# First batch of a two-layer graph network: where message work stands among the leaf products, and when the x parts of the quarters are put in

## The chip, the cores and the metric

The kernel runs on one core of one Trainium2 chip. The metric is device time in microseconds (us). Every kernel was run several times, always with runs of the kernel before on the same chip. PE is the matrix engine, DVE the vector engine, ACT the scalar engine, POOL the general-purpose engine. "Clock" is the clock that the throttle granted to PE, 1.00 being full speed.

## The reference, cut to what matters

There are 64 graphs of 256 nodes with 256 channels, all in fp32. Layer 0 adds three things into a gated unit: a convolution over the nodes (a 1-wide one, then a 17-wide one), a message pass, and the old state. Layer 1 (not touched here) normalises and aggregates over the adjacency.

```python
h = relu(bn(conv1d(xc, conv1_w, 0)))                  # xc: x with channels first
x_conv = transpose(relu(bn(conv1d(h, conv2_w, 8)) + xc))
s = x @ w_se.T + b_se                                 # 3 coordinates per node
A = exp(-squared_distances(s)) * mask                 # "distances", "mask"
msg = relu(x @ w_msg.T + b_msg)                       # "messages"
x_nmp = A @ msg                                       # "passing"
# r, z, n gates from concat(x_conv, x_nmp) and x; then layer 1
```

The 17-wide convolution is done for eight graphs (a batch) at a time by a transform: DVE splits the input into leaves, PE multiplies the leaves by transformed filters ("leaf products"), DVE merges the results back ("the way back", its additions and subtractions called butterflies in the code). The way back hands over its result in four parts, the quarters. PE transposes ("turns") each quarter into a pair of banks into which it has already put the old x of the same nodes (the "x part"). The convolution of a later batch is hidden among the gates of the batch before it. The first batch has nothing to hide among: its whole transform stands open at the start of the run, with the filters ahead of it. The change is about this opening.

## The kernel before

The parts that matter here are below. A leaf group takes three PSUM banks out of eight; `take` copies its sums away and frees them. The scheduler is manual: each engine runs its instructions in the order in which the program issues them.

```python
def products(b, first, sums):
    p1, p2, p3 = bank("ps_k1"), bank("ps_k2"), bank("ps_k3")
    ...                                        # 12 matmuls (24 records in the trace)
    def take():
        k1 = sl(sums, 2).rearrange("p s e -> p (s e)")
        nc.scalar.copy(k1, p1)                 # ACT, L395
        nc.vector.tensor_sub(..., k1, p3)      # DVE, L396
        nc.vector.tensor_add(..., k1, p2)      # DVE, L397
    return take

# in conv(b): the eight groups (four, two, one, "last")
for i, (make, after) in enumerate(todo):
    ...
    take = make()
    yield PE_WEIGHT                # before: early work is placed HERE, ahead of the take
    ...
    take()
    yield beyond * 2 * cost(2)
    if after and b == 0:
        yield from after           # the merges that follow this take, on DVE
    ...
STAGE[b] = "inverse"
...                                # butterflies (DVE)
if b == 0:
    def turned_x(q): ...           # PE puts x itself into the two banks of quarter q
    yield None
    held = [turned_x(0), turned_x(1)]
    for q in range(4):
        ...                        # second, third (DVE), then PE adds the turned quarter (L554)
        if q < 2:
            held.append(turned_x(q + 2))
        yield None
    return

def messages(k, idle=False):
    for m in range(C):
        ps = bank("ps_msg")
        for c in range(C):
            nc.tensor.matmul(ps[:, :D + 4], XT[k][:, c, m * P:(m + 1) * P], wms[:, c, :], ...)     # L626
        if idle:
            nc.tensor.matmul(ps[:, :D + 4], ones[0:1, :], bms[0:1, :], start=False, stop=True)     # L629
            nc.scalar.copy(twice[:, m, :, 0:3], ...)                                               # L630
            nc.scalar.activation(MSG[k][:, m, :], ps[:, :D], AF.Relu)                              # L631
    ...                                        # five small POOL operations

early = deque([lambda: messages(0, True), lambda: messages(1, True), lambda: factors(0), lambda: messages(2, True),
               lambda: distances(0), lambda: factors(1), lambda: distances(1)])
while STAGE.get(0) != "inverse":
    if next(first) == PE_WEIGHT and early:
        early.popleft()()
...
nc.gpsimd.tensor_add(brzn[:, :2 * D], brzn[:, :2 * D], bhh)
early.extend([lambda: mask(0), lambda: passing(0)])
for t in first:
    if t is None and early:
        early.popleft()()
mask(1)
```

`messages(k)` needs the transposed x of graph k, which was written to memory and is read back.

Of the kernel before, what the change touches and what calls it, by code (L numbers as in the profile page):

```python
# [16 lines left out]
P = 128  # L17
B, N, D = 64, 256, 256
C = D // P
# [9 lines left out]
M, T = 16, 32  # L29
# [15 lines left out]
PE_WEIGHT = 0.3  # L45
# [30 lines left out]
def gnn_two_layers(  # L76
# [17 lines left out]
    nc = tc.nc  # L94
# [4 lines left out]
    def bank(name):  # L99
        return psum.tile([P, 512], F32, tag="ps", name=name)  # L100
# [14 lines left out]
    def x_by_tiles(b, nodes, tag="xb"):  # L115

        t = conv_pool.tile([P, 4, D], F32, tag=tag, name="xb", bufs=2 if tag == "xb" else 1)
        nc.sync.dma_start(
            out=t, in_=x[b * BG:(b + 1) * BG].rearrange("g (t j) d -> (g t) j d", j=M)[:, nodes, :])
        return t  # L120
# [12 lines left out]
    ident = const.tile([P, P], F32)  # L133
# [32 lines left out]
    W2, FIRST = {}, {}  # L166
# [73 lines left out]
    def sl(a, n, step=1):  # L240
        return X[:, a:a + n] if step == 1 else X[:, a:a + (n - 1) * step + 1:step]

    def cost(n):

        return 0.15 + 0.265 * n
# [109 lines left out]
    def butterflies(pairs):  # L355
        for o, a, b, n, add in pairs:
            (nc.vector.tensor_add if add else nc.vector.tensor_sub)(sl(o, n), sl(a, n), sl(b, n))  # L357
            yield cost(n)
# [71 lines left out]
    def conv(b):  # L430
# [59 lines left out]
        for i, (make, after) in enumerate(todo):  # L490
            if i == 4:
                for t in other:
                    yield beyond * t
            take = make()
            yield PE_WEIGHT
            while vector and spent < share * (i + 1):
                t = next(vector[0], None)
                if t is None:
                    vector.popleft()
                else:  # L500
                    spent += t
                    yield beyond * t
            take()
            yield beyond * 2 * cost(2)
            if after and b == 0:
                yield from after
            elif after:
                vector.append(after)
        STAGE[b] = "inverse"
        for steps in vector:  # L510
            yield from steps
        sv, s8, s4 = sv[8, 0], s8[4, 0], s4[2, 0]
        yield from butterflies([(S2, U, U + 1, 1, True), (S2 + 1, U, U + 1, 1, False),
                                (U, S2, U + 2, 2, True), (U + 2, S2, U + 2, 2, False)])
        for j in range(2):
# [4 lines left out]
        def second(j):  # L520
            stt(sl(U + j, 2, 4), sl(U + 8 + j, 2, 4), s8[j], sl(S2 + j, 2, 4))
            yield cost(2)
            stt(sl(U + 8 + j, 2, 4), sl(U + 8 + j, 2, 4), -s8[j], sl(S2 + j, 2, 4))
            yield cost(2)
# [7 lines left out]
        for g in range(BG):  # L532
            XC[b * BG + g] = (xcs[g // 4], g % 4)
        if b == 0:

            def turned_x(q):
                xb = FIRST["xb"][q] if q < 3 else x_by_tiles(b, slice(q, M, 4))
                pss = [bank("ps_xc") for _ in range(C)]
                for o in range(C):
                    for j in range(4):  # L540
                        nc.tensor.matmul(pss[o][:, j * P:(j + 1) * P], xb[:, j, o * P:(o + 1) * P], ident,
                                         start=(j == 0), stop=False)
                return pss

            yield None
            held = [turned_x(0), turned_x(1)]
            for q in range(4):
                yield from second(q)
                yield from third(q)
                yield from third(q + 4)  # L550
                pss = held.pop(0)
                for o in range(C):
                    for j in range(4):
                        nc.tensor.matmul(pss[o][:, j * P:(j + 1) * P], X[:, V + q + 4 * j, o * P:(o + 1) * P], ident,  # L554
                                         start=False, stop=(j == 3))
                for o in range(C):
                    pv = pss[o].rearrange("p (j g t) -> p j g t", j=4, g=BG)
                    for h in range(2):
                        nc.scalar.activation(xcs[h][:, o].rearrange("p g (t j) -> p j g t", j=M)[:, q::4],
                                             pv[:, :, 4 * h:4 * h + 4, :], AF.Relu)  # L560
# [4 lines that stand above are left out]
# [18 lines left out]
        for q in range(4):  # L583
            xb = x_by_tiles(b, slice(4 * q, 4 * q + 4))
# [33 lines left out]
    def messages(k, idle=False):  # L618

        MSG[k] = ahead.tile([P, C, D], F32, tag="msg", name="msg", bufs=3)  # L620
        st = sts[k % len(sts)]
        twice = st.rearrange("p m (r e) -> p m r e", e=SR)
# [3 lines that stand above are left out]
                nc.tensor.matmul(ps[:, :D + 4], XT[k][:, c, m * P:(m + 1) * P], wms[:, c, :],  # L626
                                 start=(c == 0), stop=(c == C - 1 and not idle))
            if idle:
                nc.tensor.matmul(ps[:, :D + 4], ones[0:1, :], bms[0:1, :], start=False, stop=True)  # L629
                nc.scalar.copy(twice[:, m, :, 0:3], ps[:, D:D + 3].unsqueeze(1).to_broadcast([P, 2, 3]))  # L630
                nc.scalar.activation(MSG[k][:, m, :], ps[:, :D], AF.Relu)  # L631
                continue
            nc.vector.tensor_add(twice[:, m, :, 0:3], ps[:, D:D + 3].unsqueeze(1).to_broadcast([P, 2, 3]),
                                 bms[:, D:D + 3].unsqueeze(1).to_broadcast([P, 2, 3]))
            nc.vector.tensor_add(MSG[k][:, m, :], ps[:, :D], bms[:, :D])  # L635
        if not idle:
            nc.scalar.activation(MSG[k], MSG[k], AF.Relu)  # L637

        sq = ahead.tile([P, C, 3], F32, tag="sq", name="sq", bufs=2)
        ns = ahead.tile([P, C], F32, tag="ns", name="ns", bufs=3)  # L640
        nc.gpsimd.tensor_mul(sq, st[:, :, 0:3], st[:, :, 0:3])
        nc.gpsimd.tensor_add(ns, sq[:, :, 0], sq[:, :, 1])
        nc.gpsimd.tensor_add(ns, ns, sq[:, :, 2])
        nc.gpsimd.tensor_scalar(twice[:, :, :, 3], ns.unsqueeze(2).to_broadcast([P, C, 2]), -0.5, None, ALU.mult)
        nc.gpsimd.tensor_scalar(ns, ns, -1.0, None, ALU.mult)
        ST[k] = (st, ns)

    def factors(k):
        st, ns = ST[k]
        ps = bank("ps_sT")  # L650
        for m in range(C):
            nc.tensor.transpose(ps[:ROWS, m * P:(m + 1) * P], st[:, m, :ROWS], ident)
        lr = ahead.tile([ROWS, 2, N], F32, tag="lr", name="lr", bufs=1)
        nc.scalar.activation(lr[:, 0, :], ps[:ROWS, :N], AF.Identity, bias=lone[:, 1:2], scale=lone[:, 0:1])
        nc.scalar.copy(lr[:, 1, :], ps[:ROWS, :N])
        ST[k] = (lr, ns)

    def distances(k):
        lr, ns = ST[k]
        AT[k] = ahead.tile([P, C, N], F32, tag="AT", name="AT", bufs=2)  # L660
        pss = [bank("ps_dist") for _ in range(C)]
        for m in range(C):
            r = slice(m * SR, m * SR + 4)
            nc.tensor.matmul(pss[m][:, :N], lr[r, 0, m * P:(m + 1) * P], lr[r, 1, :], start=True, stop=True)
        for m in range(C):
            nc.scalar.activation(AT[k][:, m, :], pss[m][:, :N], AF.Exp, bias=ns[:, m:m + 1], scale=2.0)  # L666

    def mask(k):
        nc.vector.tensor_mul(AT[k], AT[k], ADJ[k])

    def passing(k):
        NMP[k] = work.tile([P, C, N], F32, tag="nmp", name="nmp")
        ps = bank("ps_nmp")
        for d in range(C):
            for m in range(C):
                nc.tensor.matmul(ps[:, d * N:(d + 1) * N], MSG[k][:, m, d * P:(d + 1) * P], AT[k][:, m, :],  # L676
                                 start=(m == 0), stop=(m == C - 1))
        nc.scalar.copy(NMP[k].rearrange("p c n -> p (c n)"), ps)
# [128 lines left out]
    first = conv(0)  # L807
# [69 lines left out]
    for k in range(3):  # L877
# [3 lines left out]
    nc.gpsimd.tensor_scalar(wrr, wrr, 0.5, None, ALU.mult)  # L881
    nc.gpsimd.tensor_scalar(brel, brel, 0.5, None, ALU.mult)

    early = deque([lambda: messages(0, True), lambda: messages(1, True), lambda: factors(0), lambda: messages(2, True),
                   lambda: distances(0), lambda: factors(1), lambda: distances(1)])
    while STAGE.get(0) != "inverse":
        if next(first) == PE_WEIGHT and early:
            early.popleft()()
    first_pool.close()

    work = ctx.enter_context(tc.tile_pool(name="work", bufs=2))
# [5 lines left out]
    nc.gpsimd.tensor_add(brzn[:, :2 * D], brzn[:, :2 * D], bhh)  # L897
    load_x(0)

    early.extend([lambda: mask(0), lambda: passing(0)])  # L900
    for t in first:
        if t is None and early:
            early.popleft()()
    mask(1)

    POINTS = 10
# [107 lines left out]
```

## Time and profile before

The opening, read from the timeline of the kernel before (us from the start of the span):

| point | us |
|---|---|
| first leaf product on PE | 80.71 |
| first take on DVE (group 0) | 99.57 |
| group 3's take on DVE | 124.54 |
| first turned quarter on PE | 163.31 |
| first gate product (L692) | 178.28 |
| total, median of the first three runs | 2303.77 |

From the first gate product on PE is nearly always busy, so the question of the change is how early that product starts. In the timeline each row is: start, length, engine, source line, operation, output<-inputs, shapes, number of instructions joined, and in brackets how long the engine stood idle before and what ended that. A chain row has start, length and what. A windows row has stretch, length, then busy time of PE, PEld, DVE, ACT and POOL, the clock, the DMA share and GB/s. One fp32 matmul shows as two records.

### The profile page before, as it was taken

The numbers are of one execution on the slowest core, as the hardware profiler recorded it, in microseconds if no ns is written. First come the engines' busy times: TensorE is split into PE (matmuls) and PEld (weight loads), VectorE is DVE, ScalarE is ACT, GpSimd is POOL, SyncE is SP. The second block draws the span as 40 slices with busy tenths as digits, with TensorE's granted clock in tenths as the row PEclk, the third lists the DMA queues.
The fourth block names the chain that finished last, engine by engine and source line by source line (L and its number), as shares of the span: only waits on it lengthen the run. The fifth ranks groups of instructions, "written<-read, shape, count | busy, mean of one in ns | idle before, by whom it ended". The sixth has DMA issues, their size and how long they took to land.

```text
span 2300.6 us, 24425 instructions
## 1 busy us (share of the span) xinstructions
PE 2230.2 (97%) x8370; PEld 1464.9 (64%) x8370; DVE 1678.8 (73%) x3188; ACT 766.4 (33%) x1585; POOL 464.7 (20%) x926
## 2 busy tenths in 40 slices
PE   8879999999999999999999999999999999999996
PEld 5665666666666666666766566666666666666663
DVE  6693988659893888839987597957889298874543
ACT  6414322442235322343224432243223532243332
POOL 0100312212122222203212121222222122121211
PEclk9889999999999999999999999999999999999998
DMA  5922242224332144222522243231432314321100
GB/s 145 310 83 78 92 144 86 86 71 142 106 96 96 47 133 137 74 97 61 175 71 81 96 133 120 73 110 51 137 121 86 101 37 154 112 79 37 46 23 14
DMA packets 212665, 226.68 MB, mean 99 GB/s; under 512 B 22087, under 2 KB 203838, under 8 KB 212542
## 3 DMA queue, kind: packets, MB, share of 16 engines
q1 hardware_dynamic: 189984, 191.14, 26.4%
q10 hardware_dynamic: 22558, 33.99, 4.2%
q8 instruction: 67, 1.10, 0.2%
q14 instruction: 56, 0.46, 0.1%
HBM read 179.22 MB, written 45.88 MB: 98 GB/s over the span
## 4 chain that ended last, share of the span: by engine, by line
PE 74%; DVE 19%; issue 2%; DMA 1%; POOL 1%; ACT 1%; SPq 1%; ACTq 0%; POOLq 0%; DVEq 0%
PE ps_rz L694 16%; PE ps_k L380 11%; PE ps_n L706 8%; PE ps_rz L692 8%; DVE XF L103 7%; PE ps_out L769 6%; PE ps_c L461 5%; PE ps_nmp L676 4%; PE ps_n L704 4%; PE ps_msg L626 4%; PE ps_out L781 3%; DVE w L103 2%; DVE bst L711 1%; DVE XF L427 1%; PE ps_xc L574 1%
## 5 line engine op out<-in xcount | busy, mean ns | idle before, releaser
L103 DVE SCALAR_TENSOR_TENSOR XF<-XF 128x512 f32<-128x512 f32 (+2 forms) x800 | 508.6, 666 | 7.4
L733 POOL TENSOR_SCALAR q<-mv 128x2 f32<-128x2 f32 x64 | 32.1, 501 | 1470.4 <-DVE mv L712 1470.4
L380 PE MATMUL ps_k<-w,XF 128*128 128x256 f32 x1316 | 301.8, 385 | 13.3 <-ACT AT L666 11.6
L380 PEld LDWEIGHTS ps_k<-w,XF 128*128 128x128 f32 x1316 | 248.7, 192 | 61.4 <-ACT AT L666 17.3
L707 DVE TENSOR_TENSOR gn<-ps_n,brzn 128x512 f32<-128x512 f32 x128 | 88.0, 688 | 239.0 <-PE ps_n L706 239.0
L698 ACT ACTIVATE rz<-rz 128x512 f32<-128x512 f32 x128 | 80.6, 630 | 508.8 <-DVE rz L697 508.8
L692 PE MATMUL ps_rz<-whh,xT 128*128 128x512 f32 x512 | 241.8, 595 | 0.0
L694 PE MATMUL ps_rz<-wih,xc 128*128 128x512 f32 x512 | 240.6, 592 | 0.0
L694 PE MATMUL ps_rz<-wih,nmp 128*128 128x512 f32 x512 | 240.6, 592 | 0.0
L769 PE MATMUL ps_out<-wrr,hT 128*128 128x512 f32 x512 | 231.9, 596 | 5.5 <-ACT hT L758 5.5
L697 DVE TENSOR_TENSOR rz<-ps_rz,brzn 128x512 f32<-128x512 f32 x128 | 87.1, 681 | 197.3 <-PE ps_rz L694 197.1
L694 PEld LDWEIGHTS ps_rz<-wih,xc 128*128 128x128 f32 x512 | 97.3, 190 | 122.5 <-issue 122.3
L694 PEld LDWEIGHTS ps_rz<-wih,nmp 128*128 128x128 f32 x512 | 97.3, 190 | 122.5 <-issue 122.5
L769 PEld LDWEIGHTS ps_out<-wrr,hT 128*128 128x128 f32 x512 | 97.8, 191 | 104.5 <-issue 89.2
L637 ACT ACTIVATE msg<-msg 128x512 f32<-128x512 f32 x61 | 38.4, 630 | 334.1 <-DVE msg L635 334.1
L626 PE MATMUL ps_msg<-wms,xT 128*128 128x260 f32 x512 | 133.6, 399 | 10.3 <-DMA w2m<-w2all 5.9
L692 PEld LDWEIGHTS ps_rz<-whh,xT 128*128 128x128 f32 x512 | 92.8, 191 | 65.0 <-issue 61.8
L704 PE MATMUL ps_n<-whh,xT 128*128 128x256 f32 x512 | 131.6, 379 | 0.0
L706 PE MATMUL ps_n<-wih,xc 128*128 128x256 f32 x512 | 131.4, 379 | 0.0
L706 PE MATMUL ps_n<-wih,nmp 128*128 128x256 f32 x512 | 131.4, 379 | 0.0
L357 DVE TENSOR_TENSOR XF<-XF 128x512 f32<-128x512 f32 (+3 forms) x128 | 125.3, 1004 | 1.7
L770 ACT COPY hr<-ps_out 128x256 f32<-128x256 f32 x128 | 47.6, 372 | 232.6 <-PE ps_out L769 232.6
(115 smaller groups left out, 3562.3 us busy)
## 6 DMA issues: line engine op xcount, KB each, us to landing
w<-w2m SPq DMA_DIRECT2D x105, 768.0 KB, 5.7
xn<-in_x_dram SPq DMA_DIRECT2D x32, 512.0 KB, 4.4
xt<-xTc ACTq DMA_DIRECT2D x32, 512.0 KB, 3.2
xT<-xt SPq DMA_DIRECT2D x64, 256.0 KB, 3.0
xb<-in_x_dram SPq DMA_DIRECT2D x32, 512.0 KB, 5.3
adj<-in_adjT_dram SPq DMA_DIRECT2D x64, 256.0 KB, 2.8
x<-in_x_dram SPq DMA_DIRECT2D x64, 256.0 KB, 3.0
out_dram<-y ACTq DMA_DIRECT2D x64, 256.0 KB, 2.2
```

The lines of the kernel that those rows point to most:

```text
L103: nc.vector.scalar_tensor_tensor(o, in0, s, in1, op0=op0, op1=op1)
L357: (nc.vector.tensor_add if add else nc.vector.tensor_sub)(sl(o, n), sl(a, n), sl(b, n))
L380: nc.tensor.matmul(ps, X[:, slot, c * P:(c + 1) * P], w(m, c), start=(c == 0), stop=(c == C - 1))
L461: nc.tensor.matmul(ps, w1[:, c, o * P:(o + 1) * P], xTc[:, c, :], start=(c == 0), stop=(c == C - 1))
L626: nc.tensor.matmul(ps[:, :D + 4], XT[k][:, c, m * P:(m + 1) * P], wms[:, c, :], start=(c == 0), stop=(c == C - 1 and not idle))
L676: nc.tensor.matmul(ps[:, d * N:(d + 1) * N], MSG[k][:, m, d * P:(d + 1) * P], AT[k][:, m, :], start=(m == 0), stop=(m == C - 1))
L692: nc.tensor.matmul(prz, XT[k][:, c, q], whh[:, c, 0:2 * D], start=(c == 0), stop=False)
L694: nc.tensor.matmul(prz, t, wih[:, i, 0:2 * D], start=False, stop=(i == 3))
L704: nc.tensor.matmul(pn[:, D:], XT[k][:, c, q], whh[:, c, 2 * D:], start=(c == 0), stop=(c == C - 1))
L706: nc.tensor.matmul(pn[:, :D], t, wih[:, i, 2 * D:], start=(i == 0), stop=(i == 3))
L707: nc.vector.tensor_add(RZ[k][1][:, n, :], pn, brzn[:, 2 * D:])
L769: nc.tensor.matmul(ps, hT[:, c, n * P:(n + 1) * P], wrr[:, c, :], start=(c == 0), stop=(c == C - 1))
```

## The change

The intent is that message work of the early graphs shall not stand in front of the leaf takes, on PE or on ACT. In numbers of groups: messages 0, messages 1, factors 0 and distances 0 go behind groups 1, 2, 3 and 4 instead of groups 0, 1, 2 and 4, and behind the take and its merges instead of ahead of it (factors is the small transpose that distances needs); messages 2, factors 1 and distances 1 go into the way back. The x parts of the first two quarters are issued ahead of the butterflies. No instruction is added or removed.

```diff
--- before.py
+++ after.py
@@ -502,14 +502,27 @@
                     yield beyond * t
             take()
             yield beyond * 2 * cost(2)
-            if after and b == 0:
-                yield from after
+            if b == 0:
+                yield from after or ()
+                yield None
             elif after:
                 vector.append(after)
         STAGE[b] = "inverse"
         for steps in vector:
             yield from steps
         sv, s8, s4 = sv[8, 0], s8[4, 0], s4[2, 0]
+        if b == 0:
+
+            def turned_x(q):
+                xb = FIRST["xb"][q] if q < 3 else x_by_tiles(b, slice(q, M, 4))
+                pss = [bank("ps_xc") for _ in range(C)]
+                for o in range(C):
+                    for j in range(4):
+                        nc.tensor.matmul(pss[o][:, j * P:(j + 1) * P], xb[:, j, o * P:(o + 1) * P], ident,
+                                         start=(j == 0), stop=False)
+                return pss
+
+            held = [turned_x(0), turned_x(1)]
         yield from butterflies([(S2, U, U + 1, 1, True), (S2 + 1, U, U + 1, 1, False),
                                 (U, S2, U + 2, 2, True), (U + 2, S2, U + 2, 2, False)])
         for j in range(2):
@@ -532,18 +545,6 @@
         for g in range(BG):
             XC[b * BG + g] = (xcs[g // 4], g % 4)
         if b == 0:
-
-            def turned_x(q):
-                xb = FIRST["xb"][q] if q < 3 else x_by_tiles(b, slice(q, M, 4))
-                pss = [bank("ps_xc") for _ in range(C)]
-                for o in range(C):
-                    for j in range(4):
-                        nc.tensor.matmul(pss[o][:, j * P:(j + 1) * P], xb[:, j, o * P:(o + 1) * P], ident,
-                                         start=(j == 0), stop=False)
-                return pss
-
-            yield None
-            held = [turned_x(0), turned_x(1)]
             for q in range(4):
                 yield from second(q)
                 yield from third(q)
@@ -881,11 +882,18 @@
     nc.gpsimd.tensor_scalar(wrr, wrr, 0.5, None, ALU.mult)
     nc.gpsimd.tensor_scalar(brel, brel, 0.5, None, ALU.mult)
 
-    early = deque([lambda: messages(0, True), lambda: messages(1, True), lambda: factors(0), lambda: messages(2, True),
-                   lambda: distances(0), lambda: factors(1), lambda: distances(1)])
+    count = 0
     while STAGE.get(0) != "inverse":
-        if next(first) == PE_WEIGHT and early:
-            early.popleft()()
+        if next(first) is None:
+            count += 1
+            if count == 2:
+                messages(0, True)
+            elif count == 3:
+                messages(1, True)
+            elif count == 4:
+                factors(0)
+            elif count == 5:
+                distances(0)
     first_pool.close()
 
     work = ctx.enter_context(tc.tile_pool(name="work", bufs=2))
@@ -897,10 +905,13 @@
     nc.gpsimd.tensor_add(brzn[:, :2 * D], brzn[:, :2 * D], bhh)
     load_x(0)
 
-    early.extend([lambda: mask(0), lambda: passing(0)])
-    for t in first:
-        if t is None and early:
-            early.popleft()()
+    early = {1: lambda: messages(2, True), 4: lambda: mask(0), 5: lambda: factors(1)}
+    later = deque([lambda: distances(1), lambda: passing(0)])
+    for i, t in enumerate(first):
+        if i in early:
+            early[i]()
+        if t is None and later:
+            later.popleft()()
     mask(1)
 
     POINTS = 10
```

In the changed kernel the lines have moved: L627 and L630 are the message matmuls (626 and 629 before), L521 the x parts (541), L555 the turned quarters (554), L693 the first gate product (692).

## The prediction

> **What bounds the kernel now.** I read the page's slices first. The matrix engine (PE) is over nine tenths busy from the fourth slice to the last but one, so nearly the whole run is PE work which this change leaves alone. Only the first three slices (57.5 us each, so to about 172 us) are below that, and there the granted clock falls too:
>
> ```profile
> PE   8879999999999999999999999999999999999996
> PEclk9889999999999999999999999999999999999998
> ```
>
> The order of instructions of the changed program, set against the old one, differs only inside this opening; the rest has the same instructions in the same order. So the question is by how much the first gate product (line 694's group; its first matmul, L692, starts at 178.44 us) comes sooner. The chain of waits, asked for 78 to 186 us, gives the opening in order (start, length, what):
>
> ```profile
> 80.42 10.73 DMA w2m<-w2all
> 91.15 1.00 issue
> 92.15 2.07 PE ps_msg L626 x4
> ...
> 121.84 1.07 PE ps_msg L626 x4
> 122.91 0.65 PE ps_msg L629 x2
> 123.58 0.16 ACT st L630
> 123.75 0.29 ACT msg L631
> 124.03 0.49 ACT XF L395
> 124.52 0.02 issue
> 124.54 0.69 DVE XF L396
> ...
> 163.31 3.96 PE ps_xc L554 x16
> ...
> 178.44 1.72 PE ps_rz L692 x4
> ```
>
> The reader should see three stretches. To 124 us the chain is PE with message work in it and a transfer ahead of it; then ScalarE (ACT) copies the messages before the leaf sums (L395); from 124.54 to 163.3 us the chain is VectorE (DVE) alone; then PE turns the quarters until the gates. The windows view shows what the transfer costs beyond its wait (stretch, length, PE busy, PEld, DVE, ACT, POOL, clock, DMA share, GB/s):
>
> ```profile
> 86.30:92.15 5.85, 0.00 (x0) 0.03 (x1) 2.79 (x4) 0.00 (x0) 0.00 (x0) 0.79 1.03 328
> 92.15:98.50 6.35, 6.35 (x12) 3.31 (x12) 0.00 (x0) 0.55 (x2) 0.00 (x0) 0.50 1.00 316
> 98.50:106.20 7.70, 7.70 (x26) 6.37 (x26) 3.43 (x6) 0.93 (x3) 1.03 (x5) 0.68 1.08 383
> 106.20:123.00 16.80, 16.80 (x74) 12.85 (x73) 10.51 (x16) 3.12 (x10) 1.04 (x5) 1.00 0.46 163
> ```
>
> PE stands 5.85 us for the first transposed x, then works at half clock. The timeline by engine adds that the first leaf sums, whose products ended at 86.29, were copied at 98.95 and used only then:
>
> ```profile
> 98.95 0.59 ACT L395 COPY XF<-ps_k 128x512 f32<-128x512 f32 x1
> 99.57 0.69 DVE L396 TENSOR_TENSOR XF<-XF,ps_k 128x512 f32<-128x512 f32 x1 [10.45 <-ACT XF L395]
> 110.55 0.69 DVE L396 TENSOR_TENSOR XF<-XF,ps_k 128x512 f32<-128x512 f32 x1 [7.44 <-ACT XF L395]
> 124.54 0.69 DVE L396 TENSOR_TENSOR XF<-XF,ps_k 128x512 f32<-128x512 f32 x1 [3.17 <-ACT XF L395]
> ```
>
> DVE loses 10.45 + 7.44 + 3.17 = 21.06 us to these three waits: the ceiling of the gain, if the rest of DVE's chain keeps its length.
>
> **What the Trainium skill says.** "TensorE: Matmul & The Clock Gate", part 1, says that PE's clock is halved after an idle window of about 3.4 us and full again after about as much work, with a free-running window. The trace agrees on the halving (0.50 after 5.85 us of idling, and message matmuls at about twice their later time) but PE stayed slow into the stretch after 98.5 us, longer than one such window. The same page, under the architectural detail, says that ScalarE and VectorE are strict FIFOs: this is why L395 stood behind message copies that had nothing to do with it, and 98.95 against 86.29 agrees. "PSUM — Partial Sum Buffer", the four rules: a matmul's output fits in one bank; with eight banks and three for each leaf group, PE can run ahead by only two groups before it needs DVE's take.
>
> **The change part by part.** I number the leaf groups 0 to 6, then the last. *Before*, PE ran group 0, message 0, group 1, message 1, group 2, factors 0, group 3, message 2 and so on. *After* it runs groups 0 and 1, message 0, group 2, message 1, group 3, factors 0, group 4, distances 0, groups 5, 6 and last, two x parts, then message 2 and factors 1; distances 1 and the first pass come among the quarters. Nothing is removed or added except order.
>
> 1. Groups 0 and 1. PE ends group 0 at 86.29 as before. A warm group is 5.35 us (24 records; 5.38 and 5.18 in the chain plus gaps), so group 1 ends at 91.64. Message 0 then finds its x nearly landed; I keep 92.15, a wait of 0.5 us, too short to cool the clock.
> 2. Message 0, warm: 106.34 to 109.55 in the chain, so 3.21 us: to 95.36. Group 2 to 100.71, message 1 to 103.92, group 3 to 109.27.
> 3. DVE starts at 89.12, the end of its last butterfly (three L357 from 86.96), as group 0's copy no longer has a message before it. A take with its small merges is 3.5 us (99.57 to 103.1), one with a size-4 merge 7.3 (110.55 to 117.85). Group 0 to 92.6, group 1 to 99.9, group 2 must wait for PE's 100.71, say 100.9 to 104.4. Group 3 must wait for 109.27, say 109.4: a new wait of 5.0 us, since two messages still stand before group 3.
> 4. So group 3's take starts at 109.4 rather than 124.54: 15.1 us sooner. Check by another way: 5.35 us of wait gone; half-clock cost of message 0 (6.43 - 3.21 = 3.2) and of the group after it (7.76 - 5.35 = 2.4); message 2 with its 3.2 and factors 0 with 0.2 no longer before group 3; and ACT's message copies, about 0.8. The sum is 15.2.
> 5. From 124.54 to 171.74 DVE before had no wait that mattered (47.2 us). After, its inputs come in time: group 3 with its long merges takes 14.9 us (124.54 to 139.43), so group 4's take starts at 124.3 when PE ended group 4 at 114.8; groups 5, 6 and last end on PE at about 120.8, 126.1 and 130.6, their takes start at 127.7, 135.0 and 138.5. The banks of group 5 need take 3 only, those of group 6 only ACT's copy of group 4. DVE is therefore unbroken, and its last third butterfly ends at 156.6 rather than 171.7.
> 6. The first quarter is ready at 148.1 (163.3 - 15.1). Message 2 and factors 1 need take 6 and the last take for their banks, so they run from about 136 to 145 even at half clock: in PE's free time ahead of 148. From the quarter to the gates before took 178.44 - 163.31 = 15.1 us, at half clock to begin with; distances 1 (four records, 0.63 us) now stands in it. So the gates start at 148.1 + 15.1 + 0.6 = 163.9.
> 7. The x parts sooner: parts 0 and 1 were done by 152.8 before the quarter at 163.3 already, so this is worth nothing by itself; it keeps them out of the later queue.
>
> Gain: 178.4 - 163.9 = 14.5 us. A somewhat warmer PE in the tail could give up to 2 us more (DVE ends at 156.6 and PE then needs only its last quarter), so I take 14.8: 2303.8 - 14.8 = **2289.0 us**, or 0.6%.
>
> **The rivals.**
> - *Messages moved, not hidden.* If message 2 came late and stood before the first quarter, it would give back up to 3 to 6 us (warm or half clock): 2292 to 2295. Against it: 3 us of room in step 6. For it: the halved clock, and two halves that share one bank, so that ACT must empty the first.
> - *DVE runs unbroken from 89 us.* Then the gain is the ceiling, 20 us or so, 2284. Against it: group 3 on PE isn't done before about 109 us.
> - *The transfer still leads.* If message 0's x lands later than I think, PE waits behind group 1; each us goes straight through to step 4, and over some 3 us cools the clock: gain 8 to 11, 2293 to 2296. For it: transfers take all the bandwidth here (386 GB/s). Against it: no transfer is moved in front of it.
> - *Taken back later.* A sooner gate could wait for its weights, adjacency or next x. Weights are issued once the last products end (about 130.7, not 145.5) and took 8.7 us, so they come before 142; I expect nothing, at most 2 us.
>
> **Range and chances.** Steps 1 to 4 are good to 2 us, the tail's clock to 2 us. The runs before lie within 0.16 us. So 2284.5 to 2293.5 should hold it 8 times in 10. 2% would be 46 us, over twice the whole ceiling: 0.01 for faster, 0.01 for slower.
>
> **What would show it.** Right: the wait before the first message under 1 us and the clock near 1 from 86 to 117 us; the first take at 89 us; one DVE wait of about 5 us before group 3's take at 109 to 110; no other DVE wait over 1 us until the quarters end near 157; the first gate near 164; from there both traces with the same differences in time. Wrong: a wait for x over 2 us behind group 1, a DVE wait for message copies in the tail, a first quarter on PE later than its DVE input, or a gate start that differs from the change in the total.

## The result, and the profile after

| | runs | median us | lowest to highest |
|---|---|---|---|
| before | 6 | 2303.19 | 2300.53 to 2303.86 |
| changed | 6 | 2288.89 | 2287.61 to 2291.63 |

The ratio is 0.9942, 95% interval 0.9929 to 0.9955. Ratios here are the mean time of one kernel's runs over that of the other's of the same rounds, so not quite the ratio of the medians. That is 13.4 us, 0.6%. The changed kernel was run again later, unaltered: 2288.30 us (2287.70 to 2289.23), ratio 0.9930 (0.9913 to 0.9947), 16 us. The text for that repeat:

> The changed kernel unaltered, for a second trace: gate at 164.8 within 0.3 us; between the gate and the end the profiled run gave back 3.0 us of its lead (13.7 at the gate, 10.7 at the end) against the trace of before. If that is chance (transfers of later weights landing differently from run to run), the loss lies elsewhere or is gone in this trace; if the change causes it, it comes back in the same batches.

The slices of the changed kernel's page, PE's busy tenths and the clock:

```profile
PE   8989999999999999999999999999999999999996
PEclk9989999999999999999999999999999999999998
```

The second slice (57 to 115 us) is fuller and warmer; the rest reads as before. The chain of the changed kernel:

```profile
91.17 1.09 issue
92.26 1.11 PE ps_msg L627 x4
...
148.53 3.96 PE ps_xc L555 x16
...
164.77 1.72 PE ps_rz L693 x4
```

No transfer leads the chain any more; what is left is a stand of 1.09 us ahead of the first message. The old chain named the transfer w2m<-w2all there, which the message does not read, and the new one names nothing. The semaphore times in the packed traces show what both waits end with: the transfer of graph 0's x lands at 91.84 us before and at 91.95 in the changed kernel, and the message starts 0.31 us later in each. The first quarter comes at 148.53 against 163.31, the first gate at 164.77 against 178.44. DVE's takes of groups 0 to 3, and ACT's first copy, in the timeline:

```profile
88.71 0.68 DVE L396 TENSOR_TENSOR XF<-XF,ps_k 128x512 f32<-128x512 f32 x1
92.15 0.68 DVE L396 TENSOR_TENSOR XF<-XF,ps_k 128x512 f32<-128x512 f32 x1
101.19 0.69 DVE L396 TENSOR_TENSOR XF<-XF,ps_k 128x512 f32<-128x512 f32 x1 [1.68 <-PE ps_k L380]
109.78 0.69 DVE L396 TENSOR_TENSOR XF<-XF,ps_k 128x512 f32<-128x512 f32 x1 [5.06 <-PE ps_k L380]
```

```profile
84.33 0.59 ACT L395 COPY XF<-ps_k 128x512 f32<-128x512 f32 x1 [3.42 <-PE ps_k L380]
```

ACT copies group 0 at 84.33 rather than 98.95. Of DVE's three old waits for ACT (10.45, 7.44 and 3.17 us) nothing is left; in their place stand two waits for PE, 1.68 and 5.06 us. The windows:

```profile
92.00:120.00 28.00, 27.74 (x122) 21.77 (x123) 20.68 (x32) 5.90 (x16) 4.57 (x10) 1.00 0.81 276
137.00:149.00 12.00, 7.64 (x19) 4.06 (x17) 11.66 (x21) 1.72 (x6) 4.34 (x7) 0.50 0.83 261
```

From 92 to 120 us PE is busy at full clock, where before it had been at half clock to 103.4. The half clock now falls in 137 to 149, where PE waits for DVE anyway, and, as before, in the first quarter behind it (to 154). DVE, busy 11.66 of 12 us, is what goes on.

**Where the gain arises.** The start of the leaf products differs from run to run (79.67 to 82.38 us over all profiles, from the filter stage ahead, which no kernel here alters), so from here on times count from that start, and "tail" is the time from the first quarter on PE to the first gate. All are read from the timeline on PE and DVE; for the changed kernel the start and the gate are these rows:

```profile
80.39 10.76 PE L380 MATMUL ps_k<-w2all,XF 128*128 128x256 f32 x48
...
164.61 1.88 PE L693 MATMUL ps_rz<-whh,xT 128*128 128x512 f32 x4
```

| kernel | group 3's take | quarter 0 on PE | first gate | tail |
|---|---|---|---|---|
| before | 43.83 | 82.60 | 97.56 | 14.97 |
| changed | 29.40 | 68.15 | 84.22 | 16.08 |
| changed, repeat | 29.11 | 67.86 | 83.69 | 15.82 |

The gain is all made by group 3's take (14.4 to 14.7 us). From there to the first quarter both take the same time, 38.77 and 38.75: DVE's chain kept its length. The tail gives back 0.9 to 1.1. At the gate 13.3 to 13.9 us are left. Two profiles of the same kernel differ by 0.2 to 0.5 us in these columns; totals of one kernel differ by up to 6.5 us between runs of one chip (the kernel before: 2300.4 to 2306.9 in a later round), so parts of 1 or 2 us are read from these columns and not from totals.

**After the gate.** The first trace of the changed kernel lost 3.0 us of the gain between gate and end: 13.67 us ahead at the gate, 10.71 at the end of the span. The repeat lost nothing: 14.05 and 14.65. One place where they differ is this one, windows of the changed kernel and then of its repeat:

```profile
1109.00:1113.00 4.00, 2.88 (x12) 1.17 (x10) 3.93 (x7) 1.42 (x4) 0.00 (x0) 1.00 0.00 0
1113.00:1117.00 4.00, 4.00 (x11) 3.23 (x12) 3.86 (x9) 0.79 (x2) 0.00 (x0) 0.57 0.00 0
```

```profile
1109.00:1113.00 4.00, 2.87 (x15) 1.96 (x12) 3.97 (x7) 1.99 (x5) 0.00 (x0) 1.00 0.00 0
1113.00:1117.00 4.00, 4.00 (x19) 3.21 (x17) 3.79 (x10) 0.00 (x0) 0.94 (x3) 1.00 0.00 0
```

In both PE stands about 1.1 us before 1113; in one the clock then drops to half for some 3.4 us (11 records against 19), in the other it does not. Between the gate and the last 30 us (where every profile has some) the first trace has three such stretches (at 840, 1113 and 1929 us), the repeat none. The kernel before has three as well (226, 854 and 1940 us); the last two stand nearly where two of the first trace stand when counted from the gate (676 and 1761 to 1764 us after it). So these stretches tell the two traces of the changed kernel apart, but not the first of them from the kernel before, and where its 3.0 us went is not settled. That they are chance of the run and not an effect of the change is what the repeat says, and the other profiles: over all fourteen, the time from gate to end lies between 2118 and 2125 us in no order that follows the edits (before 2122.3, changed 2125.2 and 2121.7, the two experiments on the kernel before 2124.8 and 2118.2).

### The profile page after: what moved, and what is told of

The parts are those of the page before. It is cut to its first block, busy times and chain, and to the rows that moved or that the text cites. A ratio compares the mean times of both kernels' runs of the same rounds, so it can differ in the third digit from the quotient of the medians.

```text
span 2289.9 us, 24427 instructions
## 1 busy us (share of the span) xinstructions
PE 2228.0 (97%) x8370; PEld 1463.0 (64%) x8370; DVE 1678.3 (73%) x3188; ACT 768.1 (34%) x1585; POOL 464.0 (20%) x926
## 4 chain that ended last, share of the span: by engine, by line
PE 79%; DVE 14%; DMA 3%; issue 2%; POOL 1%; ACT 1%; SPq 0%; ACTq 0%; POOLq 0%; DVEq 0%
PE ps_rz L695 16%; PE ps_k L380 12%; PE ps_n L707 8%; PE ps_rz L693 8%; PE ps_out L770 7%; PE ps_c L461 5%; DVE XF L103 5%; PE ps_nmp L677 5%; PE ps_n L705 4%; PE ps_msg L627 4%; PE ps_out L782 4%; DMA w<-w2m 2%; PE ps_w L225 2%; DVE w L103 1%; DVE bst L712 1%
## 5 line engine op out<-in xcount | busy, mean ns | idle before, releaser
L693 PE MATMUL ps_rz<-whh,xT 128*128 128x512 f32 x512 | 240.8, 592 | 0.0
L627 PE MATMUL ps_msg<-wms,xT 128*128 128x260 f32 x512 | 133.2, 399 | 5.8 <-DVE XF L396 4.2
L693 PEld LDWEIGHTS ps_rz<-whh,xT 128*128 128x128 f32 x512 | 92.2, 190 | 64.5 <-issue 61.2
```

The lines of the kernel that those rows point to most:

```text
L693: nc.tensor.matmul(prz, XT[k][:, c, q], whh[:, c, 0:2 * D], start=(c == 0), stop=False)
```

## The experiments

All kernels below gave correct results. Ratios are against the kernel before in the same rounds. The three rounds had medians of before of 2304.16, 2303.66 and 2304.49 us; the second round's runs of before are those of the first and one more. Where no kernel is named, the edit is to the changed kernel.

The theory was: the gain comes from taking the first message out of the path to group 3's take (its wait, the cold clock behind it, and message 2 and the ACT copies ahead of group 3), and not from the x parts. The rivals: the x parts matter; the placing behind the takes matters by itself; the way back matters; the transfer traffic and not the clock makes the slow stretch.

**1. The x parts put back.** The x parts are issued where they were, after the butterflies.

```diff
-            held = [turned_x(0), turned_x(1)]          # ahead of the butterflies
...
         if b == 0:
+            held = [turned_x(0), turned_x(1)]          # just before the quarters
             for q in range(4):
```

> The changed kernel with one part undone: the x parts of quarters 0 and 1 go back to just ahead of the quarters, behind message 2 and factors 1. My theory (PE only has to be done before DVE hands it the first quarter): nothing, first gate product at 164.8 us as in the changed kernel, within 0.5 us, total within 1 us of it. Rival (the sooner x parts are part of the gain, as the change's intent has it): the gate 2 to 4 us later, because the two parts (3.6 us at full clock, more at half) then stand right in front of the first quarter.

Measured: 2290.51 us, ratio 0.9943 (0.9926 to 0.9959); gate at 83.59, against 84.22 and 83.69. The sooner x parts are worth nothing.

**2. One group later, and nothing else.** To the kernel before: an empty entry at the head of the list, so that all message work moves by one group but stays ahead of its group's take, and message 2 stays among the leaves.

```diff
-    early = deque([lambda: messages(0, True), ...
+    early = deque([lambda: None, lambda: messages(0, True), ...
```

> The kernel before with a single edit: each piece of message work is put one leaf group later, but is still issued ahead of that group's take, so ACT copies messages before the leaf sums. Theory A (what counts is that PE has work while the first x lands and that fewer messages stand before group 3): nearly all of the gain, group 3's take at about 111.4 us (the changed kernel: 109.8), gate at about 165.5, total 12 to 13 us below before. Theory B (what counts is standing behind the takes in ACT's order): most of the gain is lost, total within 5 us of before.

Measured: 2291.87 us, ratio 0.9941 (0.9926 to 0.9957). Gate at 84.52, against 84.22 and 83.69 of the changed kernel: nearly all the gain from a single empty entry. The takes of groups 1 and 3 in its timeline:

```profile
98.35 0.69 DVE L396 TENSOR_TENSOR XF<-XF,ps_k 128x512 f32<-128x512 f32 x1 [4.15 <-ACT XF L395]
...
112.91 0.69 DVE L396 TENSOR_TENSOR XF<-XF,ps_k 128x512 f32<-128x512 f32 x1 [2.44 <-ACT XF L395]
```

DVE still waits for ACT here, with message copies ahead of the leaf copies, and group 3's take is at 30.80 rather than 29.40 and 29.11. So "behind the takes" is worth 1.4 to 1.7 us of DVE's time, of which about 1 us is made good by the shorter tail (14.97; distances 1 does not stand in it).

**3. Message 2 and its followers back among the leaves.** Messages 2, distances 0, factors 1 and distances 1 are placed behind groups 4 to 7, and the way back holds only the masks and the first pass.

```diff
             elif count == 5:
+                messages(2, True)
+            elif count == 6:
                 distances(0)
+            elif count == 7:
+                factors(1)
+            elif count == 8:
+                distances(1)
...
-    early = {1: lambda: messages(2, True), 4: lambda: mask(0), 5: lambda: factors(1)}
-    later = deque([lambda: distances(1), lambda: passing(0)])
+    early = {4: lambda: mask(0)}
+    later = deque([lambda: None, lambda: passing(0)])
```

> The changed kernel with message 2, factors 1 and distances 1 back among the leaf products, behind the takes of groups 4 to 7, so nothing of them in the way back. Theory (PE has time to spare behind group 3, and distances 1 costs its 0.6 us in the way back): gate at 164.1 us, 0.6 sooner than the changed kernel. Rival (moving message 2 to the way back is itself worth its 3.2 us of PE): gate at 168.

Measured: 2289.50 us, ratio 0.9934 (0.9919 to 0.9949), not to be told apart from the changed kernel by the total. Group 3's take is the same (29.21), the first quarter too (67.84), the gate is at 81.92, 1.8 to 2.3 us sooner, all in the tail (14.08). Distances 1 out of the tail is 0.6 of it. The rest is a warmer tail, and part of that is luck: experiment 2 has the same order of instructions in the tail and took 14.97. So moving this work into the way back gained nothing; it costs at least 0.6 us at the gate. How much above that is not settled.

**4. Messages behind group 3.** If group 3's take sets the path, the two messages still ahead of it should go too. Counts 2, 3, 4, 5 become 4, 5, 6, 7.

```diff
-            if count == 2:
+            if count == 4:
                 messages(0, True)
-            elif count == 3:
+            elif count == 5:
                 messages(1, True)
-            elif count == 4:
+            elif count == 6:
                 factors(0)
-            elif count == 5:
+            elif count == 7:
                 distances(0)
```

> The changed kernel with messages 0 and 1, factors 0 and distances 0 two groups later, so that no message stands before group 3. Theory (DVE's 5.1 us wait for group 3 and the 1.7 us for group 2 are what is left of the loss before DVE's unbroken stretch): no DVE wait over 0.5 us between 88.7 us and the quarters, group 3's take at 103.5, first quarter at about 142.3, gate at 158.6, total 6 us below the changed kernel (19 below before). Rival (a bank, the weights of the gates or the adjacency then bound the opening): gate at 162 or later.

Measured: 2280.74 us (2279.36 to 2282.72), ratio 0.9896 (0.9882 to 0.9911); repeated in another round, 2280.88 us, ratio 0.9900 (0.9885 to 0.9914).

> A repeat, on the chip of the others, of the kernel with no message before group 3: gate at 75.3 us after the first leaf product, ratio to before 0.990 (first run: 0.9896).

The takes of groups 2 and 3 in the timeline:

```profile
100.00 0.68 DVE L396 TENSOR_TENSOR XF<-XF,ps_k 128x512 f32<-128x512 f32 x1
103.44 0.68 DVE L396 TENSOR_TENSOR XF<-XF,ps_k 128x512 f32<-128x512 f32 x1
```

No wait is left: DVE runs unbroken, which is the ceiling that the prediction's second rival spoke of. Group 3's take is at 22.54 (22.75 in the repeat) against 29.40 and 29.11, and the gate at 75.27 (75.80), 7.9 to 9.0 us sooner than in the changed kernel. The take alone gives 6.4 to 6.9. About 1 us more comes because a POOL addition that slows DVE (experiment 8) now falls behind the first quarter: take 3 to quarter 0 is 37.68 rather than 38.75. This version beats both kernels, by a simple change of four numbers.

**5. What the half clock costs.** To the kernel before: PE fills its wait for the first x with six matmuls of 128 rows by 512 columns, whose result the next matmul overwrites. Wait and order stay; only the clock behind the wait differs.

```diff
             ps = bank("ps_msg")
+            for _ in range(6 if idle and k == 0 and m == 0 else 0):
+                nc.tensor.matmul(ps, ident, w1.rearrange('p c n -> p (c n)'), start=True, stop=True)
```

> The kernel before with six 128x512 matmuls of the identity on a weight, results thrown away (overwritten), ahead of message 0 in message 0's own bank: PE is busy during the wait for the first x. The wait itself stays. Theory (the half clock after the wait costs 3.2 us in message 0 and 2.4 us in the group behind it): message 0 starts at about 92.2 still, clock 1.00 from 86 to 123 us, group 3's take 5.6 us sooner, at 119, gate at 172.8, total 5.6 us below before. Rival (message 0 and its neighbour are slow because transfers take all the bandwidth): message 0 as slow as before, total as before.

Measured: 2297.08 us, ratio 0.9970 (0.9953 to 0.9987). The fill and the message behind it, in the timeline, and the window behind the fill:

```profile
87.61 5.31 PE L626 MATMUL ps_msg<-w,ident 128*128 128x512 f32 x12
93.65 1.11 PE L628 MATMUL ps_msg<-wms,xT 128*128 128x260 f32 x4 [0.72 <-issue]
```

```profile
92.30:98.70 6.40, 5.68 (x22) 3.44 (x21) 0.60 (x1) 1.48 (x5) 0.94 (x5) 1.00 0.93 274
```

The same four message matmuls take 1.11 us where they took 2.07, with the same kind of traffic (DMA share 0.93 here, 1.00 before). Group 3's take comes 5.35 us sooner than before (38.48 against 43.83) and the gate 5.74 (91.82). The step in the prediction said 3.2 + 2.4 = 5.6. The rival, that traffic slows PE there, is refuted.

**6. What the half clock in the way back costs.** Three such matmuls are put ahead of the second x part and eight behind factors 1, where PE waits for DVE anyway.

```diff
+    def warm():
+        ps = bank("ps_warm")
+        for _ in range(8):
+            nc.tensor.matmul(ps, ident, w1.rearrange('p c n -> p (c n)'), start=True, stop=True)
...
-    early = {..., 5: lambda: factors(1)}
+    early = {..., 5: lambda: (factors(1), warm())}
```

> The changed kernel with three such matmuls ahead of x part 1 and eight behind factors 1, results thrown away, so that PE doesn't stand idle from 133 to 136 and from 145 to 148.5 us. Theory (the first quarter, the next x part and distances 1 ran at half clock): first quarter at 148.5 as before but 1.8 us long, not 4.0; gate at 161.6, total 3 us below the changed kernel. Rival (PE is paced by DVE's quarters, so that the clock is hidden): gate at 164 to 165.

Measured: 2285.71 us, ratio 0.9920 (0.9905 to 0.9935). The clock is 1.00 from 137 to 164 us, and the tail is 13.75, 2.1 to 2.3 us less than in the changed kernel, not 3. The first turned quarter then takes less than its 3.96 us:

```profile
150.07 2.43 PE L557 MATMUL ps_xc<-ident,XF 128*128 128x128 f32 x16 [0.27 <-DVE XF L103]
```

It is not the 1.95 of the later quarters at full clock: it comes as DVE releases its parts. A tail at full clock is paced partly by DVE, so the full gain of a warm PE cannot be had there.

**7. Both together.** Messages behind group 3, with three such matmuls ahead of the x part and six behind factors 1.

```diff
+                for _ in range({1: 3}.get(q, 0)):
+                    nc.tensor.matmul(pss[0], ident, w1.rearrange('p c n -> p (c n)'), start=True, stop=True)
...
+        for _ in range(6):                              # warm(), behind factors 1
```

> Both: no message before group 3, and PE kept busy to the first quarter (three and six thrown-away matmuls). If the two gains add up: gate at about 155.5, total 9 us below the changed kernel, 22 us below before. If the second is already contained in the first (PE then has less idle time and might stay warm by itself): gate at 158.6, as with the first alone.

A miss: 2286.74 us, ratio 0.9922 (0.9905 to 0.9938), 6 us slower than without the fill. The fill overshot:

```profile
140.75 5.32 PE L913 MATMUL ps_warm<-w,ident 128*128 128x512 f32 x12
145.90 1.95 PE L557 MATMUL ps_xc<-ident,XF 128*128 128x128 f32 x16
```

The quarter has no wait in front of it any more: it stood behind the fill until 63.53 after the start, where it could have run at about 60.2. The tail is down to 13.27, but the 3.3 us are lost ahead of it, and the gate is at 76.80 against 75.27 and 75.80. The gate explains 1.0 to 1.5 of the 6 us. In the profiled run (2284.03 us, against 2280.9 for the profiled run without the fill) nothing is lost after the gate: its leaf products started 1.5 us later (82.38 against 80.91), its gate came 1.5 us later from there, and from gate to end it took 2123.1 against 2122.9 us. What remains is that two of its four runs took 2289.5 us; they were not profiled, so nothing says where. Of the 3.3 us some 2.6 are the three matmuls ahead of the x part (2.74 us), where PE had no wait in this version. The repair was four matmuls behind factors 1 and none elsewhere.

```diff
-        for _ in range(6):
+        for _ in range(4):
...                                                     # and no matmuls ahead of the x part
```

> The kernel with no message before group 3, plus four thrown-away matmuls behind factors 1 only (the earlier mix overshot: 3 + 6 of them held PE to 63.5 us after the first leaf product, 3.3 us past the first quarter's input). Counted from the first leaf product: quarter 0 on PE at 60.2 us as without the filling, then a tail of 13.3 us as in the mix (15.05 without): gate at 73.5 us, 1.7 us sooner than without filling, total 1.7 us lower. Rival (the tail is paced by DVE's quarters): gate at 75.

```profile
136.32 3.60 PE L911 MATMUL ps_warm<-w,ident 128*128 128x512 f32 x8
140.82 2.43 PE L555 MATMUL ps_xc<-ident,XF 128*128 128x128 f32 x16 [0.91 <-DVE XF L103]
```

PE is free 0.9 us before the quarter is there. The gate is at 74.05, 1.2 to 1.8 us sooner than without the fill, and the total is 2279.11 us (2277.05 to 2281.17), ratio 0.9890 (0.9875 to 0.9905). Against the 2280.88 of the same round that is 1.8 us less at the median, too little for totals to tell apart.

**8. A POOL addition beside DVE.** In the chain of the changed kernel one DVE operation that takes about 0.7 us elsewhere takes 1.75 (at 142.87), while POOL adds two bias rows. The timeline of the changed kernel, POOL and then DVE:

```profile
142.39 1.68 POOL L905 TENSOR_TENSOR brzn<-brzn,bhh 128x512 f32<-128x512 f32 x1 [36.44 <-DMA x<-in_x_dram]
```

```profile
142.26 2.36 DVE L103 SCALAR_TENSOR_TENSOR XF<-XF 128x512 f32<-128x512 f32 x2
```

The Trainium skill, "SBUF — State Buffer", section "Who interferes with whom", says that a DVE instruction with two SBUF inputs contends with a GpSimd instruction that reads SBUF. Both are of that kind here. To test it, the addition goes to DVE, behind the last mask.

```diff
-    nc.gpsimd.tensor_add(brzn[:, :2 * D], brzn[:, :2 * D], bhh)
...
     mask(1)
+    nc.vector.tensor_add(brzn[:, :2 * D], brzn[:, :2 * D], bhh)
```

> The changed kernel with one bias addition (128x512, 1.5 to 1.8 us on POOL, which ran at the same moment as a DVE operation that took 1.75 instead of 0.69 us in three traces) moved from POOL to DVE, behind the last mask, where DVE waits for the gate anyway. Theory (POOL and DVE share a way to SBUF, and DVE loses 1.1 us of its unbroken chain): from the first leaf product, no DVE operation at 1.75 us, quarter 0 on PE at 66.9 us rather than 68.0, gate 1 us sooner at 82.9, total 1 us lower. Rival (the 1.75 us is a semaphore or a transfer that the operation waited for, booked as its length): quarter 0 at 68.0 as before.

```profile
142.28 1.29 DVE L103 SCALAR_TENSOR_TENSOR XF<-XF 128x512 f32<-128x512 f32 x2
```

The same two operations took 1.29 us, 1.07 less, and take 3 to quarter 0 went from 38.75 to 37.69. The trace agrees with the page. The gate is at 82.65 (before this edit 84.22 and 83.69); the total, 2288.46 us, ratio 0.9930 (0.9914 to 0.9947), cannot tell it. The kernel before had the same collision (POOL 1.80 us at 157.05), so it has no part in the gain of the change. Together with the version of 7:

> No message before group 3, four filling matmuls, and the bias addition on DVE: the version that the experiments point to. From the first leaf product: quarter 0 at 60.2 (here the addition on POOL fell behind quarter 0), tail 12.5 to 13.3 us, gate at 72.7 to 73.5 us, that is 11 us sooner than the changed kernel; total about 2278, ratio to before about 0.989. If the fillings or the addition cost anything outside: no better than without them.

Measured: 2280.20 us (2276.84 to 2281.24), ratio 0.9892 (0.9877 to 0.9907), gate at 73.94 against 74.05: nothing more, as there the addition had already fallen behind the first quarter. The best that these runs reach is thus about 0.989, some 25 us, and nearly all of it is had by experiment 4 alone.

## Why the prediction was right, point by point

- **What bounds it** held: experiments 2 and 4 move group 3's take and the gate follows by nearly the same amount (against the kernel before 13.0 and 13.0 us, and 21.3 and 22.3, of which 1 us is the POOL addition).
- **Steps 1 and 2.** The wait for the message's x was put at 0.5 us and was 1.1. Group 1 ended at 91.15 rather than 91.64, and the message began at 92.26, 0.1 us later than said, or 0.4 counted from the start of the products; that much passed on to the products behind it. The clock stayed full, as said.
- **Step 3.** The first take at 89.1: 88.71. The new wait of 5.0 us before group 3: 5.06. The wait before group 2, 1.0 in the working (from 99.9 to 100.9), was 1.68.
- **Step 4.** Group 3's take at 109.4: 109.78. Its second reckoning had a sum of 15.2; the runs give 5.85 - 1.11 = 4.7 for the wait and 5.35 for the half clock (experiment 5). With message 2, factors 0 and the ACT copies at the 3.2, 0.2 and 0.8 of the prediction, which no run took singly, the sum is 14.3, against 14.4 to 14.7 measured from the start of the products.
- **Step 5.** Group 4's take at 124.3: it followed unbroken, at 124.66. Products ended at 130.6, as said.
- **Step 6.** Quarter 0 at 148.1: 148.53. The last half of an x part stood 2.87 us, to 136.13, until DVE's take of group 6 (L396), which it does not read, gave up a bank; the argument from the number of banks agrees. Message 2 ran in PE's free time, at half clock, from 137.3 to 144.1 (said: 136 to 145). From the quarter to the gate was to be 15.7 us in the chain's terms (15.1 + 0.6): it was 16.24 (148.53 to 164.77), at half clock to begin with, as before.
- **Step 7** held: experiment 1.
- **The rivals.** Message 2 did not hold up the first quarter (PE stood 3.82 us for DVE between them), the wait for the transfer was 1.1 us rather than over 3, DVE was not unbroken (experiment 4 makes it so, and gains some 23 us where that rival named 20), and of two traces one shows nothing taken back later.
- **The signs.** The clock, the first take, the wait before group 3 and the first gate came as the list of signs has them. Three did not quite: the wait before the first message was 1.1 us and not under 1, DVE had a second wait over 1 us (1.68, before group 2), and the first trace (not the repeat) lost 3.0 us after the gate.
- **The sum.** 14.8 us was said. The gate came 13.3 to 13.9 us sooner from the start of the products, the ratio of the first rounds is 13.4 us, that of the second 16. The mechanism stands; the terms that were sized too favourably are group 3's take (15.1 us sooner was said, 14.4 to 14.7 measured from the start of the products), the tail (0.6 us longer was said, 0.9 to 1.1 measured) and the 0.3 us allowed for a warmer tail, which did not come in the changed kernel. That the median fell within 0.2 us of 2289.0 is partly luck: the median of before moved by 0.6 as more of its runs came in, and the statement that the runs before lie within 0.16 us rested on three runs. Later rounds spread over 6 us.

What stays open: how much of the 2 us of experiment 3 is order and how much the clock's luck, where two of the four runs of the overfilled version of experiment 7 lost 5 us (the runs lie at 2284 and at 2289.5, and only one of the faster was profiled), and where the first trace of the changed kernel lost 3.0 us after the gate.

## What to carry to other kernels

Find the first instruction of the longest unbroken chain (here the take of group 3, with DVE busy for 39 us behind it) and put nothing in front of it on any in-order queue that feeds it, PE and ACT alike; what else must be done goes where that engine stands and waits. A wait on PE costs more than its length: here 5.85 us of standing brought 5.4 us of half clock behind it. Filling such a wait with thrown-away matmuls can pay, but the fill must end before its follower is ready: four matmuls fitted where nine, three of them in a place without a wait, lost what they had gained.

## What the Trainium skill lacked or had wrong

- "TensorE: Matmul & The Clock Gate", Part 1, gives the time to full clock as one busy window of about 3.4 us, and does not say what counts as busy beyond a word on transposes. In the kernel before PE worked from 92.15 on and was busy for all of 93.2 to 103.4 us, and the clock stayed at 0.50 to 103.4, three windows of 3.4 us; the first two of them held message matmuls and their one-row bias matmuls for the most part. In experiment 5 the same messages came behind a fill and stayed at 1.00. Whether the kind of matmul is the cause was not tested, and one case speaks against it as the only one: in the repeat of the changed kernel a half-clock stretch that held the end of an x part and then message matmuls ended after 3.4 us (136.3 to 139.7). It also has the clock halved after an idle window of about 3.4 us. A stand of 2.74 us (before, to 150.89) was enough: the x part behind it ran at 0.57. A stand of 2.87 us ahead of an x part was followed by half clock in both traces of the changed kernel, and not in experiment 8. In the long stretch after the gates a stand of about 1.1 us was followed by half clock in one run and not in another, so shorter stands count too, in some runs, and cost about 1.7 us each (an estimate: 3.4 us at half clock); for such short stands the page gives no length.
- "SBUF — State Buffer", "Who interferes with whom", gives the rule for two SBUF inputs but no cost for this pair: a POOL addition of 128x512 (1.68 us) lengthened one 128x512 DVE operation from 0.69 to 1.75 us, 1.06 us in all.
